# Two rows of a sample per partition and four 64x64 matmul tiles in a gathered matmul with residual

## The chip, the core and the metric

The kernel runs on one core of a Trainium2 chip. A core has five engines with a program of their own each: TensorE (PE in the profile, with its weight loads as PEld), VectorE (DVE), ScalarE (ACT), GpSimd (POOL) and SyncE (SP). They synchronize through semaphores. Data moves between the device memory (DRAM) and the on-chip memory (SBUF, 128 partitions) by 16 DMA engines, which are fed here from two queues, one written by ACT and one by SP. Matmul results land in PSUM, a second on-chip memory of 128 partitions, from which DVE copies them on.

The metric is the device time of one execution in microseconds, the median of the runs. The program before took 322.81 us (322.81 to 323.15 in 3 runs).

## The reference

A batch of 128 samples, each a 128x1024 matrix in fp32. Every sample has a subject number between 0 and 7, and every subject a 128x128 matrix. Each sample is multiplied by its subject's matrix, and the sample itself is added as a residual:

```python
# x (128, 128, 1024) f32, itok_B_0_7 (128,) int32, L0_cond_weights (8, 128, 128) f32
w = weights[subjects]
out = jnp.einsum('bct,bcd->bdt', x, w)
x = x + out
```

Read and written are 67.1 MB each, and the matrices are another 0.5 MB. The matrix is chosen by data, so the subject numbers are read into registers on the chip.

## The kernel before

The batch is worked through in 32 units of four samples (`NT = 32`; line 115 on sets up the buffers). One buffer `x_all` has 12 slots (`SLOTS`), each for one unit: 128 partitions, on partition c row c of each of the four samples, 4 KB a row and 16 KB a unit. The sum is formed in place, so a slot holds first the input and then the output of its unit.

**Loads** (`load`, issued by ACT, line 67). One transfer for each sample, 512 KB. The DRAM side is written as `(a r) t -> a (r t)` with `ROWS = 4`: 32 pieces of 16 KB, each four consecutive rows. The SBUF side is 128 rows of 4 KB. ACT issues them in order, and from unit 12 on waits until the unit that held the slot has been stored.

**Matmul** (`multiply`, line 174). For each half of a unit (two samples) PE waits for the weights (`s_go`) and the data (`s_ready`, raised by POOL when a unit's loads have landed) and does four matmuls of 128x128 weights by 512 columns, eight for a unit, into one of two PSUM tensors `ps`.

**Add** (`add`, line 186). DVE adds the 128x2048 result in PSUM to the same samples in the slot. **Place** (`place`, line 165): DVE copies the chosen matrices of the next unit out of `w_all` into `ws`.

**Stores** (SP, line 67; the first at line 251). One transfer of 2 MB a unit, in the last 12 units one of 4 MB for two (`PAIR`). On the SBUF side a piece is a partition's 16 KB of a unit, in the last six units (`WHOLE`) 32 KB of two. On the DRAM side the rows of 4 KB are scattered to their samples. Between units 8 and 24 a store is held back by four units (`BEHIND`).

At the start the matrices are loaded in one transfer of 128 rows of 4 KB and put in order by two transposes and 16 copies on DVE and POOL, and PE does three matmuls on zeros (`IDLE`).

A transfer's access pattern is written as a list of dimensions for each side, with the slowest first. The helper `transfer` hands the patterns on as they are written.

Of the kernel before, what the change touches and what calls it, by code (L numbers as in the profile page):

```python
# [25 lines left out]
F32 = mybir.dt.float32  # L26
I32 = mybir.dt.int32
ALU = mybir.AluOpType


G = 2
H = 2

N = 512

SLOTS = 12

P_SLOTS = 2

BEHIND = 4  # L40

EARLY = 8
LAST = 8

PAIR = 2
WHOLE = 6

DMA = 16

SORTED = 18  # L50

IDLE = 3

ROWS = 4

# [25 lines left out]
def kernel(  # L81
# [7 lines left out]
    nc = tc.nc  # L89
    B, C, T = x.shape  # L90
    S, _, D = weights.shape
    NT = B // (G * H)

    def sbuf(name, *shape, dtype=F32):
        return ctx.enter_context(nc.sbuf_tensor(name, list(shape), dtype)).ap()


    room = -(nc.sbuf_base + -nc.sbuf_base % 32) % ALIGN
    if room:
        sbuf("room", C, room // 4)  # L100
    x_all = sbuf("x_all", C, SLOTS * H * G * T)
    xs = [
        x_all[:, i * H * G * T : (i + 1) * H * G * T].rearrange("c (q t) -> c q t", t=T)
        for i in range(SLOTS)
    ]
    w_all = sbuf("w_all", C, S, D)
    w_raw, w_mid, w_late = (xs[SLOTS - 1][:, q, :] for q in range(3))
    ws = [sbuf(f"w{i}", C, 1, D) for i in range(H * G)]
    zeros = sbuf("zeros", C, N)
    given, near, wrap = (sbuf(name, 1, B, dtype=I32) for name in ("given", "near", "wrap"))  # L110
    index = sbuf("index", 1, B + H * G, dtype=I32)
    ps = [
        ctx.enter_context(nc.psum_tensor(f"ps{i}", [D, G, T], F32)).ap() for i in range(P_SLOTS)
    ]
# [4 lines left out]
    s_zeros = tc.alloc_semaphore("s_zeros")  # L119
    s_product = tc.alloc_semaphore("s_product")  # L120
    s_added = tc.alloc_semaphore("s_added")

    s_ready = tc.alloc_semaphore("s_ready")
    s_go = tc.alloc_semaphore("s_go")

    s_slot = [tc.alloc_semaphore(f"s_slot{k}") for k in range(SLOTS)]
    s_head = tc.alloc_semaphore("s_head")
    s_sort = tc.alloc_semaphore("s_sort")

    def emptied(i):  # L130
        turns = i // SLOTS
        return DMA * (H * G + 1) * turns - (DMA * G if i >= SLOTS and i % SLOTS == 0 else 0)

    def load(engine, i, q):
# [17 lines left out]

    def subjects_of(i):
        _, subject = nc.values_load_multi_w_load_instructions(
            index[0:1, i] if isinstance(i, slice) else index[0:1, bass.ds(i * (H * G), H * G)],
            engines=[mybir.EngineType.DVE],
            min_val=0,
            max_val=S - 1,
            skip_runtime_bounds_check_because="the index is clamped on the chip above",
        )  # L160
        return subject

    def place(h, subject):
        for q in range(h * G, (h + 1) * G):
            copy = nc.vector.tensor_copy(ws[q], w_all[:, bass.ds(subject[q], 1), :])  # L165
        copy.then_inc(s_go, 1)

    def multiply(slot, h):
        nc.tensor.wait_ge(s_go, 1).then_inc(s_go, -1)
        nc.tensor.wait_ge(s_ready, 1).then_inc(s_ready, -1)  # L170
        for q in range(h * G, (h + 1) * G):
            for t in range(0, T, N):
                at = slot * (H * G * T) + (q * T + t)
                mm = nc.tensor.matmul(  # L174
                    ps[h][:, q % G, t : t + N],
                    ws[q][:, 0, :],
                    x_all[:, bass.ds(at, N)],
                    start=True,
                    stop=True,
                )  # L180
        mm.then_inc(s_product, 1)

    def add(slot, h):
        mine = x_all[:, bass.ds(slot * (H * G * T) + h * G * T, G * T)]
        nc.vector.wait_ge(s_product, 1).then_inc(s_product, -1)  # L185
        nc.vector.tensor_tensor(  # L186
            mine, ps[h].rearrange("d g t -> d (g t)"), mine, ALU.add
        ).then_inc(s_added, 1)

    with tc.tile_critical():  # L190

        nc.sync.dma_start(
            w_raw, weights.rearrange("s (u j) d -> (s u) (j d)", j=S)
        ).then_inc(s_wall, DMA)
        nc.sync.dma_start(given, subjects.rearrange("(o b) -> o b", o=1)).then_inc(s_given, DMA)

        nc.vector.memset(zeros, 0.0).then_inc(s_zeros, 1)  # L197
        nc.tensor.wait_ge(s_zeros, 1)
        for _ in range(IDLE):
            nc.tensor.matmul(  # L200
                ps[P_SLOTS - 1][:, G - 1, :N], zeros[:, :D], zeros, start=True, stop=True
            )

        nc.vector.wait_ge(s_wall, DMA)
        nc.vector.transpose(  # L208
            w_mid.rearrange("p (e h w j) -> p j h e w", e=S, h=4, w=4), w_raw
        ).then_inc(s_sort, 1)  # L210
# [6 lines left out]
        nc.vector.tensor_tensor(index[:, :B], near, wrap, ALU.add).then_inc(s_index, 1)  # L217
        for i in range(NT):
            if i == SLOTS - 1:
                nc.scalar.wait_ge(s_sort, SORTED)  # L220
            if i >= SLOTS:
                nc.scalar.wait_ge(s_slot[i % SLOTS], emptied(i))
            for q in range(H * G):
                load(nc.scalar, i, q)

        nc.vector.wait_ge(s_sort, 1)
        nc.vector.transpose(w_late, w_mid).then_inc(s_sort, 1)  # L227

        def sort(engine, o, v):
            engine.tensor_copy(  # L230
                w_all[32 * v : 32 * (v + 1), 2 * o : 2 * (o + 1), :],
                w_late[32 * o : 32 * (o + 1)].rearrange("c (e v d) -> c v e d", v=4, d=D)[:, v],
            ).then_inc(s_sort, 1)

        nc.vector.wait_ge(s_sort, 2)
        nc.gpsimd.wait_ge(s_sort, 2)
        for o in range(4):
            for v in range(4):
                sort(nc.gpsimd if v == 3 else nc.vector, o, v)
        for i in range(NT):  # L240
            if i == 0:
                nc.gpsimd.wait_ge(s_head, DMA * G).then_inc(s_ready, 1)
                nc.gpsimd.wait_ge(s_slot[0], DMA * G).then_inc(s_ready, 1)
            else:
                nc.gpsimd.wait_ge(s_slot[i % SLOTS], emptied(i) + DMA * H * G).then_inc(s_ready, H)

        for i in [*range(NT - SLOTS), *range(NT - SLOTS, NT, PAIR)]:
            n = 1 if i < NT - SLOTS else PAIR
            nc.sync.wait_ge(s_added, (i + n + (BEHIND if EARLY <= i < NT - LAST else 0)) * H)
            if i == 0:  # L250
                nc.sync.dma_start(
                    out[: H * G].rearrange("g d t -> d g t"), xs[0]
                ).then_inc(s_slot[0], DMA)
            elif i + n < NT:
                store(i, n).then_inc(s_slot[i % SLOTS], DMA)


        nc.vector.wait_ge(s_index, 4)
        nc.vector.wait_ge(s_sort, SORTED)
        subject = subjects_of(slice(0, H * G))  # L260
        for h in range(H):
            place(h, subject)
        with nc.vector.Fori(0, NT) as turn:  # L263
            subject = subjects_of(turn + 1)
            for h in range(H):
                add(turn % SLOTS, h)
                place(h, subject)
        with nc.tensor.Fori(0, NT) as turn:
            for h in range(H):
                multiply(turn % SLOTS, h)  # L270

    with tc.tile_critical() as waits:
        for i in range(NT - SLOTS, NT - PAIR, PAIR):
            nc.scalar.wait_ge(s_slot[i % SLOTS], emptied(i + SLOTS))
    last = store(NT - PAIR, PAIR)

    tc.add_manual_dep(
        last.ins,
# [31 lines left out]
```

## Time and profile before

| | before |
|---|---|
| median of 3 runs | 322.81 us (322.81 to 323.15) |
| span of the profiled execution | 320.9 us |
| PE busy | 248.9 us (78%), 518 matmul records |
| DVE busy | 172.6 us (54%) |
| DMA moved | 134.76 MB, mean 420 GB/s over the span |
| DMA queue q10 (the loads, from ACT) | 6144 packets, 67.12 MB |
| DMA queue q1 (stores, matrices, subject numbers, from SP) | 4658 packets, 67.64 MB |

The profiled execution's span runs from its first to its last instruction, and the measured median lies 1.9 us above it. A busy share is an average over the span. In the row of DMA shares each digit is one fortieth of the span in tenths, and 9 means 90% or more. The packets of a queue are the data pieces and, beside them, small ones of a few bytes by which a DMA engine reports that its part of a transfer is done.

### The profile page before, as it was taken

What the parts mean: (1) busy time and instruction counts of PE and PEld (TensorE: products, weight loads), DVE (VectorE), ACT (ScalarE), POOL (GpSimd) and SP (SyncE); (2) the same over time, 40 slices, a digit from 0 to 9 for tenths busy, and PEclk for the clock granted to TensorE, in tenths of its full rate; (3) what the DMA queues carried; (4) which work ended last, traced back from release to release, by engine and by line L of the source; (5) the groups of instructions that cost most, each with busy time, mean ns of one, the idle gap of its engine ahead of it and who ended that gap; (6) DMA issues with size and microseconds to landing.
All of it is one profiled execution on the core that took longest, in us unless ns stands there. A gap on an engine that the chain in (4) does not pass through costs nothing. (4 is left out here: it accounts for less than half of the span.)

```text
span 320.9 us, 2386 instructions
## 1 busy us (share of the span) xinstructions
PE 248.9 (78%) x518; PEld 102.8 (32%) x518; DVE 172.6 (54%) x216; POOL 1.9 (1%) x8
## 2 busy tenths in 40 slices
PE   6199999999997699998498469988599957874000
PEld 2134444444433244443133224333244422331000
DVE  4636776777676167775435362675367745066000
POOL 0200000000000000000000000000000000000000
PEclk9679999999999599999789797999799989599555
DMA  7999999999999999999999999999999999999996
GB/s 294 425 425 412 426 423 432 429 423 425 425 425 425 425 424 425 425 429 425 429 435 431 427 427 429 425 425 425 425 425 425 425 425 425 427 427 455 429 445 274
DMA packets 10803, 134.76 MB, mean 420 GB/s; under 512 B 2481, under 2 KB 2482, under 8 KB 3122
## 3 DMA queue, kind: packets, MB, share of 16 engines
q1 hardware_dynamic: 4658, 67.64, 49.7%
q10 hardware_dynamic: 6144, 67.12, 49.6%
q14 instruction: 1, 0.01, 0.0%
HBM read 67.63 MB, written 67.11 MB: 420 GB/s over the span
## 5 line engine op out<-in xcount | busy, mean ns | idle before, releaser
L174 PE MATMUL ps<-x_all,w 128*128 x512 | 243.8, 635 | 42.0 <-PEq L170 34.3
L186 DVE TENSOR_TENSOR x_all<-ps,x_all 128x2048 f32 x64 | 146.7, 2292 | 117.3 <-DVEq L185 117.3
L174 PEld LDWEIGHTS ps<-x_all,w 128*128 128x128 f32 x512 | 100.9, 203 | 185.2 <-issue 184.6
L165 DVE COPY w<-w_all 128x128 f32 x132 | 23.2, 219 | 0.8 <-DVE w_all L230 0.8
L200 PE MATMUL ps<-zeros 128*128 128x512 f32 x6 | 5.2, 1033 | 1.7 <-DVE zeros L197 1.7
L230 DVE COPY w_all<-x_all 32x256 f32<-32x256 f32 x12 | 3.9, 326 | 0.4
L208 DVE STREAM_TRANSPOSE x_all<-x_all 128x1024 f32<-128x1024 f32 x1 | 2.0, 1992 | 3.1 <-DMA x_all<-in_L_cond_weights_dram 3.1
L200 PEld LDWEIGHTS ps<-zeros 128*128 128x128 f32 x6 | 1.8, 328 | 3.7 <-issue 2.1
L230 POOL COPY w_all<-x_all 32x256 f32<-32x256 f32 x4 | 1.7, 425 | 8.3 <-DVE x_all L227 8.1
L227 DVE STREAM_TRANSPOSE x_all<-x_all 128x1024 f32<-128x1024 f32 x1 | 1.2, 1225 | 0.0
L197 DVE MEMSET zeros<- 128x512 f32 x1 | 0.5, 485 | 1.0 <-SPq L190 1.0
L217 DVE CUSTOM_DVE_ANT_0 index<-near,wrap 1x256 uint16<-1x256 uint16 x1 | 0.3, 280 | 0.0
L215 DVE TENSOR_SCALAR wrap<-near 1x128 int32<-1x128 int32 x1 | 0.2, 215 | 0.0
L213 DVE TENSOR_SCALAR near<-given 1x128 int32<-1x128 int32 x1 | 0.2, 205 | 0.0
L297 POOL MEMSET const-bfloat16-1.0<- 128x1 bf16 x1 | 0.1, 100 | 0.0
L297 POOL MEMSET const-float32-0.0<- 128x1 f32 x1 | 0.1, 98 | 0.2 <-issue 0.2
L297 POOL MEMSET const-uint8-127<- 128x1 uint8 x1 | 0.1, 98 | 0.0
L297 POOL MEMSET const-float32-1.0<- 128x1 f32 x1 | 0.1, 97 | 0.0
L297 DVE BASE_LOAD x1 | 0.0, 21 | 0.1
L211 DVE MEMSET index<- 1x4 int32 x1 | 0.1, 62 | 0.0
## 6 DMA issues: line engine op xcount, KB each, us to landing
x_all<-in_x_dram ACTq DMA_DIRECT2D x128, 512.0 KB, 34.2
out_dram<-x_all SPq DMA_DIRECT2D x20, 2048.0 KB, 18.3
out_dram<-x_all SPq DMA_DIRECT2D x6, 4096.0 KB, 30.3
x_all<-in_L_cond_weights_dram SPq DMA_DIRECT2D x1, 512.0 KB, 3.7
given<-in_itok_B_dram SPq DMA_DIRECT2D x1, 0.5 KB
```

Of the source, the lines that this page charges most:

```text
L165: copy = nc.vector.tensor_copy(ws[q], w_all[:, bass.ds(subject[q], 1), :])
L174: mm = nc.tensor.matmul(ps[h][:, q % G, t : t + N], ws[q][:, 0, :], x_all[:, bass.ds(at, N)], start=True, stop=True,)
L186: nc.vector.tensor_tensor(mine, ps[h].rearrange("d g t -> d (g t)"), mine, ALU.add).then_inc(s_added, 1)
L197: nc.vector.memset(zeros, 0.0).then_inc(s_zeros, 1)
L200: nc.tensor.matmul(ps[P_SLOTS - 1][:, G - 1, :N], zeros[:, :D], zeros, start=True, stop=True)
L208: nc.vector.transpose(w_mid.rearrange("p (e h w j) -> p j h e w", e=S, h=4, w=4), w_raw).then_inc(s_sort, 1)
L213: nc.vector.tensor_scalar(near, given, -S, S - 1, ALU.max, ALU.min).then_inc(s_index, 1)
L215: nc.vector.tensor_scalar(wrap, near, 0, S, ALU.is_lt, ALU.mult).then_inc(s_index, 1)
L217: nc.vector.tensor_tensor(index[:, :B], near, wrap, ALU.add).then_inc(s_index, 1)
L227: nc.vector.transpose(w_late, w_mid).then_inc(s_sort, 1)
L230: engine.tensor_copy(w_all[32 * v : 32 * (v + 1), 2 * o : 2 * (o + 1), :], w_late[32 * o : 32 * (o + 1)].rearrange("c (e v d) -> c v e d", ...
L297: nc = _bacc.Bacc("TRN2", target_bir_lowering=False, num_devices=1)
```

## The change

A partition now holds two consecutive rows of a sample (`R = 2`), so a sample takes 64 partitions and 8 KB of each, and two samples lie side by side on the 128 partitions. A unit is still four samples. The buffers for input and output are now separate: `x_in` with 4 slots and `x_out` with 8.

**Loads.** Two transfers of 1 MB a unit instead of four of 512 KB: one with samples 0 and 2 of the unit, one with 1 and 3. The DRAM side has the dimensions 2 (the samples, two apart) x 32 (pieces of four rows) x 16 KB; the SBUF side 128 rows of 8 KB. A load waits until DVE has taken the slot's unit out of PSUM (`s_eaten`). The matrices are loaded on ACT's queue, ahead of the samples.

**Matmul.** A sample's product is cut in 64x64 weight tiles: two row halves `r`, accumulated in PSUM, by two output halves `e`, by two column blocks of 512, that is 8 matmuls a sample and 32 a unit. The four tiles that follow one another (`p`, `h`) lie on different halves of the array's rows and columns and belong to the four samples.

**Residual.** An identity, built at the start by POOL into `same`, is added to the chosen matrix when it is placed (`place` is now a `tensor_tensor` of 64x256, four a unit), so the product is already the sum. DVE then only copies 128x1024 out of PSUM, four times a unit.

**Stores.** One of 2 MB a unit, from unit 20 on (`WHOLE = 12`) one of 4 MB for two. In `x_out` a partition holds samples 0 and 1, or 2 and 3, side by side in the partitions' halves. SBUF pieces are 16 KB, or 32 KB for two units; DRAM pieces are 8 KB. `BEHIND` is 3, `IDLE` 8.

In the program of ACT, which writes the load queue, before the change (after some branches):

```order
L67 DMA x_all<-in_x_dram 128x1024 x44
L67 DMA x_all<-in_x_dram 128x1024 [waits s_sort]
L67 DMA x_all<-in_x_dram 128x1024 x3
L67 DMA x_all<-in_x_dram 128x1024 [waits s_slot0]
L67 DMA x_all<-in_x_dram 128x1024 x3
```

and at the same place after it (`x_out` holds the raw matrices at the start):

```order
L68 DMA x_out<-in_L_cond_weights_dram 64x8x256
L68 DMA x_in<-in_x_dram 128x1x2048 x8
L68 DMA x_in<-in_x_dram 128x1x2048 [waits s_eaten]
L68 DMA x_in<-in_x_dram 128x1x2048
L68 DMA x_in<-in_x_dram 128x1x2048 [waits s_eaten]
```

The 44 loads that went out without a wait are now 8, each twice as large, behind the matrices, and the wait on the store has become one on DVE's copy.

In the program of PE, one turn of its loop before (one unit):

```order
L174 ISA [waits s_go,s_ready]
L174 MATMUL ps<-x_all,w 128x512
L174 ISA
L174 MATMUL ps<-x_all,w 128x512
L174 ISA
L174 MATMUL ps<-x_all,w 128x512
L174 ISA
L174 MATMUL ps<-x_all,w 128x512
L174 ISA [waits s_go,s_ready]
```

and the first unit and a half of a turn after it (a turn is now four units):

```order
L197 MATMUL ps<-x_in,w 64x512 [waits s_go,s_ready,s_free]
L197 MATMUL ps<-x_in,w 64x512 x15
L197 MATMUL ps<-x_in,w 64x512 [waits s_free]
L197 MATMUL ps<-x_in,w 64x512 x15
L197 MATMUL ps<-x_in,w 64x512 [waits s_go,s_ready,s_free]
L197 MATMUL ps<-x_in,w 64x512 x15
```

A unit has 32 matmuls instead of 8, waits once for its data instead of twice for each half's go-ahead, and waits for PSUM by halves.

The core of the diff:

```diff
+IN = 4
+OUT = 8
-BEHIND = 4
+BEHIND = 3
-WHOLE = 6
+WHOLE = 12
-IDLE = 3
+IDLE = 8
...
+    A = C // R
+    Q = P * H
+    NT = B // Q
+    SIZE = R * T
+    BANKS = SIZE // N
...
+    def load(i, p):
+        at = (i % IN * P + p) * SIZE
         transfer(
             nc,
-            engine,
-            xs[i % SLOTS][:, q, :],
-            x[i * H * G + q].rearrange("(a r) t -> a (r t)", r=ROWS),
-        ).then_inc(s_head if i * H * G + q < G else s_slot[i % SLOTS], DMA)
+            nc.scalar,
+            x_in[:, at : at + SIZE].rearrange("c (o f) -> c o f", o=1),
+            x[i * Q : (i + 1) * Q].rearrange("(h p) (b r) t -> p h b (r t)", p=P, r=ROWS)[p],
+        ).then_inc(s_in[i % IN], DMA)
...
     def store(i, n):
-        at = i % SLOTS * H * G * T
+        at = i % OUT * P * SIZE
         return transfer(
             nc,
             nc.sync,
-            out[i * H * G : (i + n) * H * G].rearrange("g d t -> d g t"),
-            x_all[:, at : at + n * H * G * T].rearrange(
-                "d (o t) -> d o t", o=1 if i >= NT - WHOLE else n
-            ),
+            out[i * Q : (i + n) * Q].rearrange("(g h) (a r) t -> (h a) g (r t)", h=H, r=R),
+            x_out[:, at : at + n * P * SIZE].rearrange("a (o f) -> a o f", o=1),
         )
...
+    def place(u, subject):
+        return [
+            nc.vector.tensor_tensor(
+                ws[u][p][h * A : (h + 1) * A],
+                w_all[h * A : (h + 1) * A, bass.ds(subject[h * P + p], 1), :],
+                same[h * A : (h + 1) * A],
+                ALU.add,
+            )
+            for p in range(P)
+            for h in range(H)
+        ]
...
+        for b in range(BANKS):
+            if b % 2 == 0:
+                nc.tensor.wait_ge(s_free, 1).then_inc(s_free, -1)
+            e, t = divmod(b * N, T)
+            for r in range(R):
+                for p in range(P):
+                    for h in range(H):
+                        rows = slice(h * A, (h + 1) * A)
+                        at = (i % IN * P + p) * SIZE + r * T + t
+                        mm = nc.tensor.matmul(
+                            ps[h][p * A : (p + 1) * A, b],
+                            ws[i % 2][p][rows, 0, r * D + e * A : r * D + (e + 1) * A],
+                            x_in[rows, at : at + N],
+                            start=r == 0,
+                            stop=r == R - 1,
+                        )
+            if b % 2 == 1:
+                mm.then_inc(s_product, 1)
+
+    def copy(slot, p, half):
+        at = slot * (P * SIZE) + (p * SIZE + half * T)
+        return nc.vector.tensor_copy(
+            x_out[:, bass.ds(at, T)],
+            ps[p][:, half * (T // N) : (half + 1) * (T // N)].rearrange("d b n -> d (b n)"),
+        )
...
+        for i in range(NT):
+            if i >= IN:
+                nc.scalar.wait_ge(s_eaten, i - IN + 1)
+            for p in range(P):
+                load(i, p)
...
+        for i, n in stores[:-1]:
+            nc.sync.wait_ge(s_added, i + n + (BEHIND if EARLY <= i < NT - LAST else 0))
+            store(i, n).then_inc(s_out[i % OUT], DMA)
```

More of the change, by code (lines that the diff above doesn't have):

```diff
@@ L169, in multiply @@
+    def multiply(i):
         nc.tensor.wait_ge(s_go, 1).then_inc(s_go, -1)
         nc.tensor.wait_ge(s_ready, 1).then_inc(s_ready, -1)
[L171 to L180, printed above, removed]
@@ L247 @@
[L247 to L255, printed above, removed]
+            if i - OUT in stored:
+                n, count = stored[i - OUT]
+                nc.gpsimd.wait_ge(s_out[i % OUT], count).then_inc(s_room, n)
@@ L263 @@
[L263 to L270, printed above, removed]
+            sort(h)
+        nc.vector.wait_ge(s_sort, H)
+        nc.vector.wait_ge(s_same, H)
+        for u in range(2):
+            placed = place(u, subject[u * Q : (u + 1) * Q])
+            placed[0].then_inc(s_free, 1)
+            placed[-1].then_inc(s_go, 1)
@@ new lines @@
+        with nc.vector.Fori(0, NT // 2) as turn:
+            for u in range(2):
+                subject = subjects_of(bass.ds(turn * (2 * Q) + (u + 2) * Q, Q))
+                slot = (turn * 2 + u) % OUT
+                nc.vector.wait_ge(s_room, 1).then_inc(s_room, -1)
+                for half in range(2):
+                    nc.vector.wait_ge(s_product, 1).then_inc(s_product, -1)
+                    for p in range(P):
+                        copied = copy(slot, p, half)
+                        if half and not p:
+                            copied.then_inc(s_eaten, 1)
+                    copied.then_inc(s_free, 1)
+                placed = place(u, subject)
+                placed[0].then_inc(s_added, 1)
+                placed[-1].then_inc(s_go, 1)
@@ L272 @@
+        with nc.tensor.Fori(0, NT // IN):
+            for i in range(IN):
+                multiply(i)
     with tc.tile_critical() as waits:
[L273 to L275 removed]
+        for i, n in stores[:-1]:
+            if i >= NT - OUT:
+                nc.scalar.wait_ge(s_out[i % OUT], stored[i][1])
+    last = store(*stores[-1])
     tc.add_manual_dep(
```

133 lines of the change are left out of this document (59 added, 74 removed).

## The prediction

> **What bounds the kernel now.** I read the page's DMA rows first, because the kernel moves 134 MB and computes little with them. The row of digits is the mean busy share of the 16 DMA engines in 40 slices of the span; q10 is the load queue, q1 holds the stores, the matrices and the subject numbers. The last number of a queue's row is the time its packets took, as a share of sixteen engines' span.
>
> ```profile
> span 320.9 us, 2386 instructions
> DMA  7999999999999999999999999999999999999996
> GB/s 294 425 425 412 426 423 432 429 423 425 425 425 425 425 424 425 425 429 425 429 435 431 427 427 429 425 425 425 425 425 425 425 425 425 427 427 455 429 445 274
> DMA packets 10803, 134.76 MB, mean 420 GB/s; under 512 B 2481, under 2 KB 2482, under 8 KB 3122
> q1 hardware_dynamic: 4658, 67.64, 49.7%
> q10 hardware_dynamic: 6144, 67.12, 49.6%
> ```
>
> The two queues together fill 99.3% of all sixteen engines' time. So the time is the work of the DMA engines, 318.7 us, and some 2 us at the ends. The engines that compute have room. These rows are groups of instructions (busy time, mean of one, idle time before them) and waits (total, times, longest):
>
> ```profile
> L174 PE MATMUL ps<-x_all,w 128*128 x512 | 243.8, 635 | 42.0 <-PEq L170 34.3
> L186 DVE TENSOR_TENSOR x_all<-ps,x_all 128x2048 f32 x64 | 146.7, 2292 | 117.3 <-DVEq L185 117.3
> L165 DVE COPY w<-w_all 128x128 f32 x132 | 23.2, 219 | 0.8 <-DVE w_all L230 0.8
> PE ps L174 <- PEq L170: 34.3, 12, 4.6
> ```
>
> PE waits at line 170 (for a unit's data) again and again, and DVE is idle for 117 us before its adds. Neither sets the end. What the change does to the DMA engines decides.
>
> **How a transfer is spread over the engines.** The page counts packets, and the program says how many transfers there were, with how many pieces each:
>
> ```profile
> x_all<-in_x_dram ACTq DMA_DIRECT2D x128, 512.0 KB, 34.2
> out_dram<-x_all SPq DMA_DIRECT2D x20, 2048.0 KB, 18.3
> out_dram<-x_all SPq DMA_DIRECT2D x6, 4096.0 KB, 30.3
> x_all<-in_L_cond_weights_dram SPq DMA_DIRECT2D x1, 512.0 KB, 3.7
> given<-in_itok_B_dram SPq DMA_DIRECT2D x1, 0.5 KB
> ```
>
> The 128 loads have 32 pieces of 16 KB each, 4,096 pieces; q10 has 6,144 packets, so 2,048 are left, 16 for each load. These are the reports of the engines that took part. All queues together have 2,481 packets under 512 bytes. With sixteen for each of the 128 loads, the 26 stores and the matrices that is 155 x 16 = 2,480. The one left belongs to the subject numbers, whose pattern has a single row of 512 bytes (the one packet between 512 bytes and 2 KB). So transfers whose slowest dimension counts 32 or 128 were shared by sixteen engines, and the one that counts 1 went to one engine. The piece count follows the slowest dimension in both kinds.
>
> In the changed loads the slowest dimension on the DRAM side is the pair of samples, two apart: it counts 2, and 32 pieces of four rows come under it. The two cannot be one dimension of 64, since the samples are not neighbours. If an engine gets a share of the slowest dimension, as these rows suggest, a load of 1 MB goes to two engines, one for each sample, and the other fourteen carry stores alone.
>
> The Trainium skill's page "DMA: Bandwidth & Descriptors" (section "Why a DMA increments its semaphore by 16 and not by 1") says that the number of engines is the largest one up to 16 that divides the counts of both sides' slowest dimension above 1, on SP's and ACT's queues the lowest-numbered ones. The count of reports here agrees at 32, 128 and 1; no run here shows 2. By the rule the sum is the one of the next part, by a reading that counts all 64 pieces the DMA work stays at 318 us.
>
> **The change, part by part.** First the rate of one engine. At the end, from 296 us on, only stores run:
>
> ```profile
> DMA packets 339, 9.54 MB, mean 381 GB/s; under 512 B 48, under 2 KB 48, under 8 KB 48
> q1 hardware_dynamic: 339, 9.54, 89.4%
> ```
>
> 89.4% of 25 us on 16 engines is 357.6 us for 9.54 MB: 26.68 GB/s for one engine. Over the whole span the queues' shares give the same within 2%, reports included.
>
> - *Loads on two engines.* From q10's share they take 0.496 x 16 x 320.9 = 2,547 us of engine time, reports of sixteen included; at 26.68 GB/s their 67.12 MB take 2,516. I take the middle, 2,530, since the reports shrink to two a load: 1,265 us on each of the two.
> - *Stores stay on sixteen.* Their slowest dimension is the 128 partitions on both sides. From q1's share 2,552 us, at the tail's rate 2,515 for 67.1 MB; the middle over 16 is 158 us on each engine. The pieces of 8 KB instead of 4 KB in DRAM and the 32 KB pieces in six more units may shave a little: rows for large and small pieces differ by under 2%, within the ends just named.
> - *The two engines' work*: 1,265 + 158 = 1,423 us, without a pause, since loads stand ahead: four slots hold eight loads of 1,265 / 64 = 20 us each, and only the matmuls and copies of one unit (below, 17 + 5 us) must pass before a slot is refilled, under the 120 us that the other three give. The new wait on `s_eaten` therefore costs nothing; behind it on ACT stand only loads. BEHIND and the eight output slots cost nothing for the same reason: a unit comes every 44 us, and 2 MB of store are done in a fraction of that on fourteen engines, in about 10 us on the two, where its eight pieces alternate with those of loads.
> - *Start.* The first slices of 0.15 us up to 6 us:
>
> ```profile
> DMA  0000000000000930154499989999998999779097
> ```
>
>  Nothing moves in the first 13 slices (2 us), and the engines are full at about slice 24: 3.6 us. The matrices now go ahead of the samples, on 64 rows, on the same queue; 0.5 MB over sixteen engines is 1.2 us and within this. The affine selects on POOL, two copies of the matrices on DVE and the eight warm-up matmuls lie under the first unit, which needs 40 us to arrive; without that cover the two copies would show, about 2.3 us each at line 186's 2,292 ns for 2,048 columns.
> - *DVE and PE in the loop.* Four copies of 1,024 columns at half of 2,292 ns and four small placements at about the 219 ns of line 165 (ends: 219 and the 326 ns of the start's 32x256 copies) are 5.5 to 6 us a unit, beside 44 us of loads. PE has 32 matmuls a unit, each as two records (before: 256 matmuls, 512 records). How long it takes is only seen at the end.
> - *The last unit.* These rows are of PE in the first unit and of its weight loads, one a record, in order of time, then a late unit, and the last store's issue:
>
> ```profile
> 14.54 9.84 PE L174 MATMUL ps<-x_all,w 128*128 x16 [7.71 <-DVE w L165]
> 15.55 0.33 PEld L174 LDWEIGHTS ps<-x_all,w 128*128 128x128 f32 x1 [0.52 <-issue]
> 16.40 0.33 PEld L174 LDWEIGHTS ps<-x_all,w 128*128 128x128 f32 x1 [0.52 <-issue]
> 20.35 0.19 PEld L174 LDWEIGHTS ps<-x_all,w 128*128 128x128 f32 x1 [0.24 <-issue]
> 20.78 0.19 PEld L174 LDWEIGHTS ps<-x_all,w 128*128 128x128 f32 x1 [0.24 <-issue]
> 285.44 7.13 PE L174 MATMUL ps<-x_all,w 128*128 x16 [1.74 <-PEq L170]
> 295.69 0.54 SPq L67 DMA_DIRECT2D out_dram<-x_all  x1
> ```
>
>  After a long pause records come every 0.85 us for some 6 us, then every 0.43 us. A 64x64 tile streams the same 512 columns, so a record should cost the same. A unit now has 64 records. If four tiles run at once they fill 16 places, 9.8 us as in the first row; two at once 32 places, 9.8 + 16 x 0.43 = 16.7; one at a time 30.5. The trace has no tiles. I take two: the two records of one matmul stand behind one another on the same tile, so if PE begins them in order, the second of one matmul can overlap only the first of the next. Then two copies (2.4), the issue (0.6) and a store: its data time is in the 158, but a transfer has about 2.5 us beside it (the matrices landed 3.7 us after issue, 1.2 of it at 427 GB/s), and 0.9 us follow the last landing (295.69 + 24.3 to 320.9; the landing is from this row of the stretch from 296 us):
>
> ```profile
> out_dram<-x_all SPq DMA_DIRECT2D x1, 4096.0 KB, 24.3
> ```
>
> The sum: 3.6 + 1,423 + 16.7 + 2.4 + 0.6 + 2.5 + 0.9 = 1,449.7 us of span. The profiled execution before had 320.9 us of span against a median of 322.81, so 1.9 more: 1,452 us, 4.5 times the time before.
>
> **Rivals.**
>
> *Sixteen engines after all, four tiles at once.* If the spread counts all 64 pieces, or two engines are picked in turn for each load, the sixteen stay full. All 134.76 MB at 26.68 GB/s are 315.7 us against 318.7 now, so the time would be 320 to 323 us: faster by up to 0.9%, or the same. For it: the engines' shares leave nothing else to win or lose. Against it: the single report of the one-row transfer, and that eight loads in flight would have to fall on different engines by turns, which a transfer with one row cannot show. It decides faster only as long as a unit's matmuls stay under 10 us (320 / 32).
>
> *Sixteen engines, and PE becomes the bound.* With two tiles at once PE needs 1,024 x 0.43 = 440 us, begins at about 14.5 us, loses 3 us until records come every 0.43 us, and 16 us follow it (copies, issue, 4 MB at 427 GB/s, ends): with the 1.9 about 476 us. For it: two records a matmul on one tile. With one at a time 881 + 34 + 2, about 917 us. Against both: they need the spread that the report count speaks against. The Trainium skill's page "TensorE: Matmul & The Clock Gate" (Part 3) says that matmuls on different tile positions run at the same time but begin and end strictly in order; no run here shows it, and it would give the 476.
>
> *Two engines, but not at the old rate.* The slices of the page from the second to the 35th lie between 412 and 435 GB/s, 3% around 425. With fourteen engines nearly idle the two could be quicker, or slower if one engine's reads of 16 KB from one sample wait more when no other is near; I allow 3% either way, 43 us.
>
> **How the numbers follow.** Two engines: 0.85, because the one transfer in the trace with a small count went to one engine. Sixteen and four tiles: 0.07 (faster 0.05, same 0.02). Sixteen and two tiles: 0.06, one tile: 0.02. The likeliest case's bounds are 3.6 + 1,415 + 9.8 + 6.4 + 1.9 = 1,437 and 3.6 + 1,433 + 30.5 + 6.4 + 1.9 = 1,475; with 3% of rate either way 1,395 to 1,520, which holds nearly all of that case. Slower 0.93, faster 0.05, same 0.02, where 0.2% (0.6 us) is about what a measurement of this kernel can tell from no change.
>
> **What would show it.** Packets under 512 bytes: 64 x 2 for the loads, 26 x 16 for the stores, 16 for the matrices and one, 561 in all, if the loads use two engines, and 1,457 if sixteen. A mean busy share near 0.22 and 93 GB/s over the span, a unit every 44 us, PE idle for 27 us in each and waiting for data, the last loads landing some 33 us before the end. Wrong would be: sixteen reports a load, DMA shares above 0.9, or PE busy without pause; then one of the other rivals holds.

## The result, and the profile after

The changed kernel takes 1427.35 us (median of 4 runs, 1426.74 to 1427.51), the kernel before in the same session 322.98 us (322.81 to 323.21): 4.42 times the time, with a 95% interval of 4.411 to 4.424. In all that follows medians are over all runs of a kernel, while ratios and their intervals leave out runs that lie well above the kernel's fastest ones, so a ratio can lie a little under the quotient of two medians.

The page of the changed kernel; the digits and GB/s are by fortieths of the span, and the last number of a queue's row is its packets' share of the time of sixteen engines:

```profile
span 1425.7 us, 5224 instructions
...
DMA  1221222212211121222221222212213116311312
GB/s 61 106 106 54 105 106 105 106 54 105 105 54 54 54 105 60 99 105 105 106 99 60 105 105 105 106 54 105 105 54 158 53 54 260 157 54 54 157 54 128
DMA packets 8503, 134.80 MB, mean 95 GB/s; under 512 B 561, under 2 KB 1074, under 8 KB 1074
...
q10 hardware_dynamic: 4752, 67.63, 11.2%
q1 hardware_dynamic: 3746, 67.11, 11.0%
...
L197 PE MATMUL ps<-x_in,w 64*64 64x512 f32 x2048 | 294.4, 736 | 1101.8 <-PEq L190 1101.8
L209 DVE COPY x_out<-ps 128x1024 f32 x128 | 150.8, 1219 | 1192.7 <-DVEq L291 1192.7
...
L175 DVE TENSOR_TENSOR w<-w_all,same 64x256 f32<-64x256 f32 x136 | 57.1, 419 | 3.1
```

The two queues now fill 22% of the engines' time instead of 99%. The 561 packets under 512 bytes are 64 x 2 for the loads, 26 x 16 for the stores, 16 for the matrices and one for the subject numbers, so each load was shared by two engines. In the slices with 54 GB/s only loads run. PE (busy 294 us on its 2,048 records) and DVE wait: PE for 1,102 us ahead of a unit's first matmul, where it waits for the weights, for the data and then (line 190) for room in PSUM. DVE makes the weights and the room and has long done so (ahead of the last unit, below, it is idle for 32 us), so what PE waits for are the data.

A stretch in which only loads run, as a row of stretches (its start, end and length, then busy time of PE, of its weight loads, of DVE and of POOL, then the granted clock, the DMA share and GB/s):

```profile
10.00:45.00 35.00, 1.70 (x4) 0.39 (x3) 2.30 (x6) 0.00 (x0) 0.56 0.13 54
```

A share of 0.13 is 2/16, two engines without a pause, at 27 GB/s each. The end of the program in order of time (start, duration, engine, line, operation and count), and the last store as the view of DMA issues has it from 1,380 us on (last number: us to landing):

```profile
1398.27 9.71 PE L197 MATMUL ps<-x_in,w 64*64 64x512 f32 x64 [30.23 <-PEq L190]
...
1400.85 0.27 PEld L197 LDWEIGHTS ps<-x_in,w 64*64 64x64 f32 x4 [0.58 <-issue]
1401.71 0.27 PEld L197 LDWEIGHTS ps<-x_in,w 64*64 64x64 f32 x4 [0.58 <-issue]
...
1404.79 0.16 PEld L197 LDWEIGHTS ps<-x_in,w 64*64 64x64 f32 x4 [0.27 <-issue]
1404.89 2.36 DVE L209 COPY x_out<-ps 128x1024 f32 x2 [32.45 <-DVEq L291]
1405.22 0.16 PEld L197 LDWEIGHTS ps<-x_in,w 64*64 64x64 f32 x4 [0.27 <-issue]
...
1408.25 2.36 DVE L209 COPY x_out<-ps 128x1024 f32 x2 [1.00 <-DVEq L291]
1410.63 1.74 DVE L175 TENSOR_TENSOR w<-w_all,same 64x256 f32<-64x256 f32 x4
1412.67 0.54 SPq L68 DMA_DIRECT2D out_dram<-x_out  x1
```

```profile
out_dram<-x_out SPq DMA_DIRECT2D x1, 4096.0 KB, 12.1
```

The last unit's data are there at 1,398 us; PE, two copies, four placements and one store of 4 MB fill the remaining 27.4 us. Weight loads, one a record, come in fours, every 0.86 us and later every 0.43 us.

### The profile page after: what moved, and what is told of

It is laid out like the page before. It is cut to its first block, busy times and chain, and to the rows that moved or that the text cites. A ratio compares the mean times of both kernels' runs of the same rounds, so it can differ in the third digit from the quotient of the medians.

```text
span 1425.7 us, 5224 instructions
## 1 busy us (share of the span) xinstructions
PE 304.5 (21%) x2064; PEld 102.0 (7%) x2064; DVE 211.7 (15%) x272; POOL 1.0 (0%) x6
## 5 line engine op out<-in xcount | busy, mean ns | idle before, releaser
L197 PE MATMUL ps<-x_in,w 64*64 64x512 f32 x2048 | 294.4, 736 | 1101.8 <-PEq L190 1101.8
L209 DVE COPY x_out<-ps 128x1024 f32 x128 | 150.8, 1219 | 1192.7 <-DVEq L291 1192.7
L197 PEld LDWEIGHTS ps<-x_in,w 64*64 64x64 f32 x2048 | 98.0, 167 | 1298.2 <-issue 1298.2
L175 DVE TENSOR_TENSOR w<-w_all,same 64x256 f32<-64x256 f32 x136 | 57.1, 419 | 3.1
L233 PE MATMUL ps<-x_out 128*128 128x512 f32 x16 | 10.0, 797 | 1.7 <-DVE x_out L230 1.7
L233 PEld LDWEIGHTS ps<-x_out 128*128 128x128 f32 x16 | 4.0, 260 | 6.8 <-issue 5.2
## 6 DMA issues: line engine op xcount, KB each, us to landing
out_dram<-x_out SPq DMA_DIRECT2D x6, 4096.0 KB, 18.5
```

The costliest lines, as they stand in the source:

```text
L175: nc.vector.tensor_tensor(ws[u][p][h * A : (h + 1) * A], w_all[h * A : (h + 1) * A, bass.ds(subject[h * P + p], 1), :], same[h * A : (h + ...
L197: mm = nc.tensor.matmul(ps[h][p * A : (p + 1) * A, b], ws[i % 2][p][rows, 0, r * D + e * A : r * D + (e + 1) * A], x_in[rows, at : at + N] ...
L209: return nc.vector.tensor_copy(x_out[:, bass.ds(at, T)], ps[p][:, half * (T // N) : (half + 1) * (T // N)].rearrange("d b n -> d (b n)"),)
L233: nc.tensor.matmul(ps[P - 1][:, BANKS - 1], zeros[:, :D], zeros, start=True, stop=True)
```

## The experiments

The theory: the time is set by the number of engines that carry the loads, and this number follows the slowest dimension (2). The rivals: reads from two samples far apart are slow in themselves, whatever the number of engines; or the rest of the rewrite (separate buffers, four input slots, quarter-array tiles, the residual in the matrices) costs something that the loads hide. Unless said otherwise, an edit is made to the changed kernel.

**Each load split by sample.** The same bytes to the same places, but 32 pieces in one dimension, which makes sixteen engines.

```diff
-            x_in[:, at : at + SIZE].rearrange("c (o f) -> c o f", o=1),
-            x[i * Q : (i + 1) * Q].rearrange("(h p) (b r) t -> p h b (r t)", p=P, r=ROWS)[p],
+        for h in range(H):
...
+                x_in[h * A : (h + 1) * A, at : at + SIZE],
+                x[i * Q + h * P + p].rearrange("(b r) t -> b (r t)", r=ROWS),
```

> Each load of two samples is split into two loads of one sample: 32 pieces of 16 KB in DRAM, 64 partitions of 8 KB in SBUF; all else as in the changed kernel. Theory (an engine gets a share of the slowest dimension, here 32 and 64, so sixteen engines): the sixteen engines carry 134.8 MB again, 316 to 319 us of work, time 318 to 330 us, packets under 512 bytes 128 x 16 + 26 x 16 + 17 = 2,481. Rival 1 (the waits: four input slots, refilled only when DVE has copied, hold the loads back): the slots are the same, so the time stays near 1,427 us. Rival 2 (PE with 64x64 tiles becomes the bound): 440 us or more; the changed kernel's 64 records of a unit in 8.6 to 9.7 us speak for under 320 us.

Measured: 380.36 us (375.27 to 399.36 in 5 runs), 1.171 times the time before (1.164 to 1.178). The page, and the stretch from 10 to 30 us, in which only loads run (columns as above):

```profile
DMA packets 10423, 134.81 MB, mean 339 GB/s; under 512 B 2481, under 2 KB 2994, under 8 KB 2994
...
q10 hardware_dynamic: 6672, 67.64, 55.4%
```

```profile
10.00:30.00 20.00, 14.38 (x107) 5.06 (x110) 9.35 (x16) 0.00 (x0) 0.83 1.03 229
```

The reports are the 2,481 of sixteen engines a load, and 1,047 us of the change are gone with this one edit: the count was the cause. But 57 us are left over the kernel before, where a return to its time was expected. Sixteen engines are full (share 1.03) and still move only 229 GB/s: something holds each of them at half its rate. It does not pass: from 124 to 144 us, again with loads alone, they move 235 GB/s. (The profile is of the longest of the five runs, 399.36 us.) A load now goes to 64 partitions in a row, the lower or the upper half. The split also doubles the number of transfers.

**Four and eight blocks.** The loads keep their two DRAM dimensions and 64 pieces of 16 KB into 128 partitions, but the slowest dimension counts 4 (16 pieces each), then 8 (8 pieces each).

```diff
-            x[i * Q : (i + 1) * Q].rearrange("(h p) (b r) t -> p h b (r t)", p=P, r=ROWS)[p],
+            x[SPAN * (i * Q // SPAN) : SPAN * (i * Q // SPAN + 1)].rearrange(
+                "s (b r) t -> s b (r t)", r=ROWS
+            )[:, PIECES * (2 * i + p) % 32 : PIECES * (2 * i + p) % 32 + PIECES],
```

> Only the DRAM side of the loads differs from the changed kernel: 4 blocks of 16 pieces of 16 KB, taken from four neighbouring samples (a sample's quarter or so each), instead of 2 blocks of 32 from two. Each partition gets other rows than its own, so the output is not the reference's; bytes, pieces, waits and all else are the same. Theory (engines by the slowest dimension, 4): loads on four engines, 2,513 / 4 = 628 us, with the stores' 158 and the 13 us at the ends that the changed kernel has beside 1,256 + 158, about 799 us; packets under 512 bytes 64 x 4 + 433 = 689. Rival 3 (a load from samples that are no neighbours, in two dimensions, is slow in itself, not by the number of engines): it is still two-dimensional and from more places, near 1,427 us or more.

> As the run with 4 blocks, but 8 blocks of 8 pieces from eight neighbouring samples (again other rows than the reference's). Theory: eight engines, 314 + 158 + 13 = 485 us, packets under 512 bytes 64 x 8 + 433 = 945. Rival 3: near 1,427 us or more.

Measured: 811.06 us with four, 513.3 us with eight. For each the page and the loads-only stretch, four first:

```profile
DMA packets 8631, 134.80 MB, mean 167 GB/s; under 512 B 689, under 2 KB 1202, under 8 KB 1202
```

```profile
10.00:30.00 20.00, 1.81 (x10) 0.60 (x12) 2.44 (x6) 0.00 (x0) 0.64 0.25 102
```

```profile
DMA packets 8887, 134.80 MB, mean 264 GB/s; under 512 B 945, under 2 KB 1458, under 8 KB 1458
```

```profile
10.00:30.00 20.00, 6.72 (x38) 2.19 (x40) 2.40 (x6) 0.00 (x0) 0.66 0.50 125
```

689 and 945 are 64 x 4 and 64 x 8 beside the same 433, and the shares 0.25 and 0.50 are 4/16 and 8/16. So the number of engines follows the slowest dimension at 2, 4 and 8. Two-dimensional reads from samples far apart are not slow in themselves: an engine gives 27 GB/s with two of them and 25.5 with four (102 / 4; from 20 to 28 us it is 109 / 4 = 27). That rival falls. With eight engines one gives only 15.6 GB/s (125 / 8) in this stretch, which none of the expectations had, and the run takes 28 us more than the 485 expected; a later stretch is shown below.

**Neighbours side by side.** Only the load changes: its two samples are now neighbours, so that the DRAM side is one dimension of 64 pieces.

```diff
-            x_in[:, at : at + SIZE].rearrange("c (o f) -> c o f", o=1),
-            x[i * Q : (i + 1) * Q].rearrange("(h p) (b r) t -> p h b (r t)", p=P, r=ROWS)[p],
+            x_in[:, at : at + SIZE],
+            x[i * Q + p * H : i * Q + (p + 1) * H].rearrange("h (b r) t -> (h b) (r t)", r=ROWS),
```

> One edit to the changed kernel: the load takes neighbouring samples (0 and 1, 2 and 3), one dimension of 64 pieces, in place of 0 and 2, 1 and 3. Stores and matrices are left as they are, so samples 1 and 2 of each unit change places and get each other's matrix; the output is not the reference's, the work is the same. Theory: sixteen engines on all transfers and all 128 partitions on both sides, 314 to 319 us of work, 316 to 324 us, and PE (64 records of a unit in under 10 us) does not bound. If the rest of the rewrite (four input slots, 64x64 tiles, copies) costs something of its own, it shows here as more than 324 us.

Measured: 341.17 us (338.71 to 342.71 in 6 runs), 1.054 times before (1.051 to 1.058). The page, and two pieces of PE's order of time:

```profile
DMA  7999999999999889999999999999999999996047
GB/s 239 432 430 427 422 430 430 428 430 432 430 430 428 354 281 432 430 430 432 430 430 432 432 430 432 432 432 428 459 405 455 430 405 429 435 449 272 4 186 308
```

```profile
69.45 7.10 PE L197 MATMUL ps<-x_in,w 64*64 64x512 f32 x64 [1.86 <-PEq L190]
...
312.77 9.67 PE L197 MATMUL ps<-x_in,w 64*64 64x512 f32 x64 [7.02 <-PEq L190]
```

Most slices run at 427 to 432 GB/s, like those of the kernel before. The 18 us over it lie in two holes: slices 14 and 15, and above all the last four, from 306 us on, with almost nothing moved between 315 and 323 us. The last unit's data are there at 312.77 us, all earlier stores are done by then, and nothing is left to move while PE (9.7 us) and DVE work on the last unit. PE is not the bound: 64 records take 7.10 us after a short pause.

**Neighbours, with tiles of 64x128.** Same loads; the weights are cut in tiles of half the rows and all columns, and the stores are those of the kernel before.

```diff
-                            ps[h][p * A : (p + 1) * A, b],
-                            ws[i % 2][p][rows, 0, r * D + e * A : r * D + (e + 1) * A],
+                            ps[p][:, h * (T // N) + t // N],
+                            ws[i % 2][p][rows, 0, r * D : (r + 1) * D],
...
-            out[i * Q : (i + n) * Q].rearrange("(g h) (a r) t -> (h a) g (r t)", h=H, r=R),
+            out[i * Q : (i + n) * Q].rearrange("g d t -> d g t"),
```

> A correct kernel in which both sides of every transfer have a slowest dimension of 64 or more: neighbouring samples loaded side by side (two rows a partition, 64 pieces of 16 KB), matmuls with 64x128 weight tiles (16 a unit, one row half of the array each), so an output row has a partition of its own again and is stored as before the change (128 partitions, 4 KB rows in DRAM, 16 or 32 KB a partition). Residual in the matrices, four input and eight output slots as in the changed kernel. Theory: sixteen engines, 315 to 319 us of work, 317 to 325 us. Rival: with row tiles alone, two at once, PE needs 32 records x 0.43 / 2 = 7 us a unit if both run, 14 us and 450 us in all if they do not.

Measured: 341.6 us (336.7 to 344.5 in 6 runs), 1.055 times (1.050 to 1.059). PE's order of time:

```profile
57.34 7.14 PE L195 MATMUL ps<-x_in,w 64*128 64x512 f32 x32 [3.25 <-PEq L189]
```

The same time as with four tiles, so neither the 64x64 tiles nor the new pattern of the stores are what is left. 32 records of 64x128, two tiles at once, take what 64 records of 64x64 take. The hole at the end stays. What both kernels share with the changed one, beside the copies and the residual in the matrices, are the four input slots.

**A ring of twelve.** The kernel with 64x128 tiles gets one ring of 12 slots for input and output, in which the output of a unit goes into the slots two behind; a load waits for the store of the unit ten earlier. `BEHIND` is 4 and PE's loop is written out.

```diff
-IN = 4
+SLOTS = 12
-OUT = 8
+SHIFT = 2
-BEHIND = 3
+BEHIND = 4
...
-            if i >= IN:
-                nc.scalar.wait_ge(s_eaten, i - IN + 1)
+            if i >= SLOTS - SHIFT:
+                nc.scalar.wait_ge(*stored[i - SLOTS + SHIFT])
```

> The kernel with 64x128 tiles, with one ring of twelve slots in place of four input and eight output slots: the output of a unit goes to the slot whose input PE has used two units earlier, a load waits for the store ten units earlier, BEHIND is 4, and PE's loop is written out. Transfers are the same. If the 18 us that the runs with sixteen engines and 128 partitions on both sides (338 to 344 us) lie above the kernel before come from the four input slots, by which the loads end at 310 us of 340 and the engines stand nearly still in slice 38 of 40 (4 GB/s): the loads end near 285 us, the hole is gone, 318 to 325 us. If they come from the tiles or the copies: 335 us or more.

Measured: 327.84 us (323.73 to 332.97 in 10 runs), 1.006 times before (1.004 to 1.008). Its page:

```profile
DMA  7999999999999999999999999999999999999976
GB/s 226 425 437 424 419 435 427 425 427 429 431 423 429 435 421 433 431 415 429 429 427 421 429 435 421 429 429 427 425 433 445 413 421 443 405 421 433 411 303 262
```

And PE's last unit:

```profile
297.96 9.25 PE L193 MATMUL ps<-x_all,w 64*128 64x512 f32 x32 [7.26 <-PEq L187]
```

The hole is nearly gone (2.6 us without a transfer are left, from 310 to 313 us), and the median falls by 13.8 us. With ten units of room the loads run further ahead of the stores: the last unit's data are there at 298 us instead of 313, though not at the expected 285, and stores are left over that cover most of its work. Ring, `BEHIND` and written-out loop were changed together; which share each has was not tried.

**The ring with pieces of 32 KB.** One edit to the last: eight rows a piece in the loads.

```diff
-ROWS = 4
+ROWS = 8
```

> As the run with the ring of twelve, with ROWS = 8: the loads' DRAM pieces are 32 KB, 32 of them in a load instead of 64 of 16 KB. If a piece costs some nanoseconds beside its bytes: 1 to 2 us less than the run with 16 KB pieces. If not: the same.

Measured: 323.81 us (323.29 to 325.32 in 11 runs), 1.0021 times before (1.0011 to 1.0032). Its page:

```profile
span 322.0 us, 3105 instructions
...
q10 hardware_dynamic: 3600, 67.64, 49.6%
q1 hardware_dynamic: 3746, 67.11, 49.1%
```

Both queues are back where the kernel before has them. The medians lie 4 us apart, but the ratios to the kernel before, 1.0059 for the ring and 1.0021 here, give 1.2 us, which is within the expectation; the rest of the 4 us is that the ring's runs spread over 9 us and these over 2, for a reason that no run here shows. This is the best version with two rows a partition, and it does not beat the kernel before, since the DMA engines' work is the same (98.7% of 322.0 us, against 99.3% of 320.9).

**Stores on two engines.** The neighbours are loaded side by side, and now each store is written with a slowest DRAM dimension of 2.

```diff
-            out[i * Q : (i + n) * Q].rearrange("(g h) (a r) t -> (h a) g (r t)", h=H, r=R),
-            x_out[:, at : at + n * P * SIZE].rearrange("a (o f) -> a o f", o=1),
+            out[i * Q : (i + 1) * Q].rearrange("(p h) (a r) t -> h p a (r t)", h=H, r=R)[part],
+            x_out[:, at : at + SIZE].rearrange("a (o f) -> a o f", o=1),
```

> The pairing is turned round: samples 0 and 1 (2 and 3) are loaded side by side, one dimension of 64 pieces, and samples 0 and 2 (1 and 3) are stored side by side, so a store (now 1 MB, two a unit, in all units) has the dimensions 2 x 64 x 8 KB on the DRAM side. Theory (the slowest dimension of either side counts, on writes too): loads on sixteen engines, stores on two, 1,256 + 158 + some 15 us, 1,420 to 1,445 us, with the waits moved from the loads to the output slots. A rival by which only reads of samples that are no neighbours are slow gives 320 to 330 us.

Measured: 1428.99 us. The page, and the stretch from 10 to 30 us, in which almost only loads run:

```profile
DMA packets 13975, 134.80 MB, mean 94 GB/s; under 512 B 1169, under 2 KB 1682, under 8 KB 1682
```

```profile
10.00:30.00 20.00, 18.91 (x174) 7.62 (x176) 15.37 (x24) 0.00 (x0) 1.00 1.00 427
```

The 1,169 reports are 64 x 16 for the loads, 64 x 2 for the stores and 17 for matrices and subject numbers. Loads alone reach 427 GB/s, and two engines for the stores cost within 2 us of what two engines for the loads cost. The rule is one of the transfer, not of reading: a count of 2 on the DRAM side decides in both directions, against 128 rows on the SBUF side. A small count on the SBUF side alone was not tried.

**Which half, or how many partitions?** Three runs on the 229 GB/s of the loads by sample. First, the loads by sample go to every other partition instead of one half; still 512 KB to 64 partitions.

```diff
-                x_in[h * A : (h + 1) * A, at : at + SIZE],
+                x_in[h :: H, at : at + SIZE],
```

> The run with one load a sample again, but each load writes 64 partitions that lie two apart, so that they span the whole 128, instead of the lower or upper 64; rows land on other partitions than their own, so the output is not the reference's. If the 380 us of that run come from writing one half of the partitions with all engines at a time: about what sixteen engines and 128 partitions gave, 338 to 345 us, and about 430 GB/s from 10 to 30 us instead of 229. If they come from loads of 512 KB or from pieces of two partitions: 375 us or more and about 229 GB/s.

Measured: 343.79 us.

```profile
10.00:30.00 20.00, 18.65 (x170) 7.58 (x172) 15.48 (x23) 0.00 (x0) 1.00 1.01 427
```

427 GB/s instead of 229 (a store begins near the end of the stretch; from 10 to 24 us, with loads alone, it is 426), with as many transfers, bytes, pieces and partitions. Writing one half of the partitions is the cause; the number of transfers is not. The 344 us are close to those of four input slots with the neighbours loaded in one (341).

Second, the loads by sample with the upper halves on SP's queue, where they stand between the stores.

```diff
-            nc.scalar,
+            nc.sync if h else nc.scalar,
```

> The run with one load a sample again (64 partitions each, sixteen engines), but the loads of the upper 64 partitions go out on SP's queue, between the stores, those of the lower 64 on ACT's, so that both halves can be written at the same time. If it was the half of the partitions that held that run at 229 GB/s on loads alone and 380 us: clearly faster, 325 to 350 us. If a load of 512 KB to 64 partitions is slow by itself (two partitions a piece, or the twofold number of loads): no better, 370 to 400 us.

Measured: 410.98 us (403.74 to 414.34 in 4 runs), 1.257 times (1.251 to 1.262).

```profile
10.00:30.00 20.00, 14.62 (x109) 5.12 (x111) 8.37 (x14) 0.00 (x0) 0.83 1.01 261
```

Both halves are asked for at once, and the rate rises from 229 to 261 GB/s only. The expected cure failed, and in the whole kernel it is worse than one queue (the profile is of the longest run, 414.34 us). In this stretch the packets of the two queues take 50.6% and 50.2% of the sixteen engines' time, about 100% together, which fits an engine that works on a piece of one queue at a time. That the engines then turn to the same half together, so that the halves still do not overlap, is argued; no view here shows it.

Third, stores cut by halves of the partitions, with the neighbours loaded in one.

```diff
-    def store(i, n):
+    def store(i, part):
...
-            x_out[:, at : at + n * P * SIZE].rearrange("a (o f) -> a o f", o=1),
+            x_out[part * A : (part + 1) * A, at : at + P * SIZE].rearrange("a (o f) -> a o f", o=1),
```

> Neighbouring samples 0 and 1 (2 and 3) are loaded side by side: 64 pieces of 16 KB in one dimension, 128 partitions. The stores are cut by partition halves instead: two of 1 MB a unit, each from 64 partitions with 16 KB a partition, to two neighbouring samples. All transfers then have a slowest dimension of 64 or 128, so sixteen engines by the theory, with 2 x 1 MB stores in all units. In the run with one load a sample, sixteen engines moved 229 GB/s from 10 to 30 us, when they wrote 64 partitions and nothing else ran, and that run took 380 us. If reading 64 partitions is held back like writing them: 360 to 400 us. If not, 316 to 319 us of work, 318 to 328 us. If sixteen engines were not reached: 1,400 us.

Measured: 352.65 us (345.72 to 358.55 in 4 runs), between the two expectations. Its page:

```profile
q1 hardware_dynamic: 5122, 67.11, 49.2%
q10 hardware_dynamic: 5648, 67.64, 46.7%
```

The stores take 49.2% of 346.7 us. The two shorter runs, 345.72 and 348.49 us, lie 5 to 7 us over the 341 of the neighbours loaded in one, so reading one half of the partitions costs far less than writing one half (39 us, 380 against 341). How much of it is the larger number of transfers was not tried.

**Eight blocks at another distance.** Back to the 15.6 GB/s of an engine: the eight blocks are read 640 KB apart instead of 512 KB.

```diff
-            x[SPAN * (i * Q // SPAN) : SPAN * (i * Q // SPAN + 1)].rearrange(
+            bass.AP(
...
+                ap=[[40 * ROWS * T, SPAN], [ROWS * T, PIECES], [1, ROWS * T]],
```

> The run with 8 blocks again, whose eight engines moved 125 GB/s from 10 to 30 us when only loads ran, 15.6 GB/s each where four engines had 102 in all, 25.5 each. Here the eight blocks of a load lie 640 KB apart in DRAM instead of 512 KB, a power of two; partitions, pieces and waits are the same (again other rows than the reference's). If the eight engines hinder one another in DRAM by that distance: about 210 GB/s from 10 to 30 us and less than 513 us in all, near 490. If they hinder one another where they write (each has 16 partitions in a row to itself): about 125 GB/s again and 505 to 520 us.

Measured: 514.07 us, the 513.3 of before within 0.2%.

```profile
10.00:30.00 20.00, 7.69 (x45) 2.57 (x48) 2.39 (x6) 0.00 (x0) 0.66 0.51 131
```

The distance in DRAM is not it. Nor are the 16 partitions in a row that each of the eight engines writes, taken by themselves. Later in the first run with eight blocks there is again a stretch with loads alone:

```profile
160.00:180.00 20.00, 16.79 (x128) 6.05 (x128) 10.20 (x14) 0.00 (x0) 0.83 0.50 215
```

The same eight engines with the same partitions move 215 GB/s, 26.9 each, as two and four engines do (the run with the other distance has 217 from 160 to 175 us). So the 15.6 GB/s belong to the start of the program and not to a transfer on eight engines; what holds the engines back there stays open.

## Why the prediction was right, point by point

It said 1,452 us and got 1,427; the mechanism was the one named, and two terms of the sum were mis-sized by more than 2 us.

- *"A load of 1 MB goes to two engines."* Right: 561 reports, the number it gave, and the share of 0.13 in the loads-only stretch. Undoing only this (loads of neighbours, 341 us) gives back 1,086 us. The trace ahead of it carried the argument thinly, with one transfer of a single row; the runs at 2, 4 and 8 show it. The Trainium skill's page "DMA: Bandwidth & Descriptors" (section "Why a DMA increments its semaphore by 16 and not by 1") has the largest number up to 16 that divides the slowest counts of both sides; the reports at 2, 4 and 8 agree with it, and at 2 for stores too. All counts tried are powers of two, so no run shows what a count like 10 or 20 would do.
- *"26.68 GB/s for one engine" and 1,423 us on the two.* Too slow by 18.5 us: the sum has the last load at 3.6 + 1,423 - 9.8 = 1,416.8 us, and the last unit's data were there at 1,398.3. Each of the two moved 33.55 MB of loads and 3.97 MB of stores and matrices by then, which is 37.5 MB in 1,394.7 us, 26.9 GB/s. At the 26.68 taken from the tail these 37.5 MB are 1,406 us; the other 7 us came from the middle with the engine time of q10, which holds sixteen reports a load, where two are left.
- *The last unit, 16.7 us for two tiles at once.* Mis-sized by 7 us: PE took 9.71 us, the value that it worked out for four tiles (9.8). Weight loads come four at a time, every 0.86, then 0.43 us, where the 128x128 records came one at a time at that pace, so the two records of a matmul on one tile did not hold up the other tiles. Whether the records stand in another order than the prediction took, or begin out of order, the rows do not show. The same error makes PE's pause in a unit 34 us instead of 27. The Trainium skill's page "TensorE: Matmul & The Clock Gate" (Part 3), read as it was there, would give two; 64 records in 7.10 us here (16 places of 0.43 to 0.44 us) do not bear that reading out.
- *The rest of the end, 16.2 us.* 17.7 were measured (1,425.7 - 1,408.0). Missing in the sum were four placements of 1.74 us: they are made after the last unit's copies too, for a unit that does not exist, and the last store's go-ahead comes behind them. The store's landing took 12.1 us against 0.6 + 9.8 + 2.5 = 12.9.
- *DVE, 5.5 to 6 us a unit.* Measured 4 x 1.22 + 4 x 0.42 = 6.6 us; the placements took 419 ns where 219 to 326 were taken. Hidden under 44 us of loads, except at the end.
- *The wait on `s_eaten` costs nothing.* Right with two engines. With sixteen the kernels with four input slots take 341 us and the ring 328, in which `BEHIND` and PE's loop are changed too, so it is likely, but not shown, that the wait costs most of the difference. The first rival's 320 to 323 us were too low by some 18 us in any case; what it left out is that the last unit's work needs stores left over to cover it.
- *PE becomes the bound (476 us).* Falls in every run with sixteen engines: 64 records need 7.1 to 9.7 us, and a unit comes every 10.
- *Two engines, but not at the old rate.* 1% faster than taken, within the 3% allowed.

## What to carry to other kernels

Count the slowest dimension of both sides of a transfer before its bytes: two neighbours can be merged into one long dimension, two samples with a gap cannot, and the transfer shrinks to as many engines as the pair counts. A repair that splits the transfer must then be looked at for the partitions it writes: 64 in a row moved at 229 GB/s, every other one of 128 at 427. In a kernel bound by transfers, ask of each smaller ring of slots what still moves while the last unit is computed.

## What the runs showed of the hardware that was not expected

- Writing one half of the partitions halves the rate of sixteen engines: 229 GB/s for loads to 64 partitions in a row, 427 for the same loads to every other partition. The Trainium skill's page "SBUF — State Buffer" (section "Door 1: The DMA port swizzle (why `[64,N]` ≈ `[32,N]`)") says that the partition number picks one of 16 ports and that the lower 64 reach only eight of them, the upper 64 the other eight; both runs agree. The loads with one half on each queue, at 261 GB/s, are not explained by the ports alone.
- Reading one half for stores costs far less than writing one half for loads (345.7 and 348.5 us in the shorter runs against 375 to 380).
- An engine moves 27 GB/s whether two, four or eight carry the loads (54, 109 and 215 GB/s with loads alone). But from 10 to 30 us of the program eight engines reached only 15.6 GB/s each with blocks 512 KB apart in DRAM, and 16.4 with blocks 640 KB apart.
- fp32 matmuls on four 64x64 tiles, each two records, run four at once: 64 records in 7.10 us, as long as 32 records on 64x128 tiles (7.14 us) and the 16 on the whole array in the kernel before (7.13 us).
- Pieces of 32 KB instead of 16 KB in the loads took 1.2 us off the ring's time by the ratios (1.0059 and 1.0021 times before), and its runs spread over 2 us instead of 9.
